# A residual's copy within DRAM, in one piece per image or in quarters, and an order account with two transfer queues

## The chip, the cores and the metric

The kernel runs on one core of a Trainium2 chip. The metric is the device time of one execution in microseconds. Before the change it is 3294.26 us, the median of three runs (3291.0 to 3302.8).

## The reference

Input x has 8 images of 256 channels and 32 x 32 positions, all in float32. Two layers follow each other.

```python
# layer 0, on the group-normalised x: convolutional attention
q = einsum("bchw,oc->bohw", x, q_w)                    # 8 heads of 32 channels, 1024 queries (and one global token)
kv = einsum("bchw,oc->bohw", x, kv_w)
ks, vs = (layernorm(pooled(t)) for t in split(kv))     # pooled: 4 sizes, 1024+256+121+25 = 1426 keys,
                                                       # each p + depthwise3x3(p)
att = softmax(q k^T * 32**-0.5) v
out = proj(att mixed over the channels of a head by a softmax made from the global token)
x = x + out                                            # the residual of layer 0
# layer 1, on the 1024 tokens of an image
t = t + softmax((LN(t) Wq)(LN(t) Wk)^T / 16) (LN(t) Wv)
t = t + sum_e w[f, e] * (relu(bn(relu(bn(LN(t) W1_e)) W2_e)) Wo_e)   # 8 experts; w: a softmax over experts
                                                       # of the mean over the images, for each token f
```

## The kernel before

`attention` computes layer 0 and the attention of layer 1; `experts` computes the experts. Both record every engine instruction through a class `Flow`, in one order per engine. That is why nearly all rows of the profile have one line, L670.

**The attention's main loop.** Layer 0 is a loop over 32 units: 8 images b, 2 groups c of four heads, 2 halves of the queries. A unit has 11 chunks kc of 128 keys; the last 18 keys of an image are taken together in one more step, so there are 360 steps in all. A step has four score matmuls into `sc` (one buffer, four PSUM banks), an exponential on ScalarE into a tile `pt` of 1 MB (six buffers), and, a step later, four matmuls into `pv`. For the softmax's denominator `add` sums two neighbouring `pt` tiles with an accumulating DMA that GpSimd (POOL) issues (`pt<-pt`, 160 of them), and `sums` on VectorE adds the pair into the unit's first pair, each half by itself. `unit`, a background thread, then normalises; after an image's last unit it starts `project`.

**The residual.** `t1[b]` is an image in DRAM. `prepare(b)`, which runs about one image ahead of the main loop, loads x[b] into SBUF (`xi`, two DMAs of 512 KB on SyncE's queue), has the copy x[b] to t1[b] issued within DRAM (1 MB, `t<-in_x_dram` in the profile) and goes on with the group norm, the pooling and the matmuls of keys, values and queries. `project(b)`, after the units of the image, adds its four quarters of 128 channels x 512 positions into t1[b] by accumulating DMAs from POOL (`t<-xr`). The last image has no such copy: `project` loads it and adds on VectorE. `layer1` then loads t1[b] (`t<-t`), and `outputs` reads it once more as its residual (`res<-t`).

**What sets the order.** `Flow` keeps an account: for each engine the time at which its last recorded instruction would end (`now`), for each tile when it is written (`ready`) and last read (`read`). `note` adds an instruction: it starts when its engine, its inputs and its output's readers allow it, lasts `cost`, and is seen by others `lag` later. Background threads (convolution, key and value tokens, projection, layer 1, its outputs) yield what they need next: an engine and tiles. `step` lets those go on whose tiles the account has ready within a few us of TensorE's time (`AHEAD`, `NEAR`), as long as a credit of matmul time per step lasts (`PACE`, `PACE1`); `finish` runs threads until a condition holds. So an estimate of a transfer's duration decides which instruction stands where on each engine, and the engines take them in this order. The chip itself waits for semaphores, not for the account.

A DMA's lag was a line for each queue: 2.0 us + 0.0045 us per KB on SyncE's, 1.5 us + 0.0078 us per KB on POOL's, whatever else was under way.

**After the attention.** While layer 1 of the last images and the gate of the experts (which needs all images) are still under way, `ahead` fills TensorE with first and second expert layers, whose results are stored in DRAM (`h<-h`) and fetched later. Expert layers of 256 x 256 weights are computed in seven products of 128 (`layer7`), except the first few, which are plain.

Of the kernel before, what the change touches and what calls it, by code (L numbers as in the profile page):

```python
# [14 lines left out]
DRAM = bass.MemoryType.DRAM  # L15

P = 128
# [7 lines left out]
NKC = 12  # L25
# [27 lines left out]
class Kit:  # L53


    def __init__(self, nc):
        self.nc = nc
        self.n = 0
# [598 lines left out]
class Flow:  # L657
# [27 lines left out]
    def __init__(self, tc, kit):  # L685
        nc = tc.nc
        self.tc, self.kit = tc, kit
        self.now = dict.fromkeys(("PE", "DVE", "ACT", "POOL", "SP"), 0.0)
        self.last = {}
        self.ready, self.read, self.writer, self.reader, self.slots, self.open = {}, {}, {}, {}, {}, set()  # L690
        self.pe = self.Engine(self, "PE", nc.tensor)
        self.ve = self.Engine(self, "DVE", nc.vector)
        self.act = self.Engine(self, "ACT", nc.scalar)
        self.pool = self.Engine(self, "POOL", nc.gpsimd)
        self.sp = self.Engine(self, "SP", nc.sync)
        self.threads = []
        self.cut = {}
        self.also = {}
        self.tiled = None
        self.columns = False  # L700
        self.credit, self.port = [0.0, 0.0], 0.0

    def tile(self, pool, shape, tag, bufs=1):
# [60 lines left out]
    def note(self, engine, op, ins, args, kwargs):  # L764
        aps = [a for a in (*args, *kwargs.values()) if hasattr(a, "tensor") or hasattr(a, "space")]
        out = kwargs.get("out", args[0] if args else aps[0])
        srcs = [a for a in aps if a is not out]
        prev = self.last.get(engine)
        if prev is not None:
            self.tc.add_manual_dep(  # L770
                ins.ins,
                prev,
                mybir.DependencyInfo(mybir.DependencyClass.NoSync, mybir.DependencyReason.DATA),
                reason="program order",
            )
        self.last[engine] = ins.ins.name
        start = self.now[engine]
        names = [n for a in srcs for n in self.keys(a)]
        outs = self.keys(out)
        for n in (*names, *outs):  # L780
            if self.writer.get(n) != engine:
                start = max(start, self.ready.get(n, 0.0))
        for o in outs:
            if self.reader.get(o, engine) != engine:
                start = max(start, self.read.get(o, 0.0))
        cost = self.cost(engine, op, out, srcs)
        if engine == "PE":

            tiling = None if op == "transpose" else self.tiling(srcs)
            if tiling != self.tiled:  # L790
                cost += {None: 0.2, "rows": 0.2, "columns": 0.13, "both": 0.2}[tiling]
                self.tiled = tiling

        wide = [a for a in srcs if a.space != PSUM and a.free_size() > 4]
        if "dma" not in op and engine == "POOL" or engine == "DVE" and wide and (len(wide) > 1 or op in ("tensor_scalar", "tensor_copy")):
            start = max(start, self.port)
            self.port = start + cost
        self.now[engine] = end = start + cost
        lag = 0.15
        if "dma" in op:  # L800
            size = 4e-3 * out.shape[0] * out.free_size() if out.space != DRAM else 4e-3 * srcs[0].shape[0] * srcs[0].free_size()
            lag = 2.0 + 0.0045 * size if engine == "SP" else 1.5 + 0.0078 * size
        for n in {*outs, self.key(out)}:
            self.ready[n] = max(self.ready.get(n, 0.0), end + lag)
            self.writer[n] = "DMA" if "dma" in op else engine
        self.open.difference_update(names)
        for n in {*names, *map(self.key, srcs)}:
            self.read[n] = max(self.read.get(n, 0.0), end + lag)
            self.reader[n] = engine

    @staticmethod
    def key(a):
# [85 lines left out]
def attention(tc, kit, f, outer, ended, nb, consts, x, t1, t2, hn, bounds, vecs, q_t, kv_t, proj_t, gqk_t, wqk, wqkv, vecs1, w1_d, w1c, gate_d, wrc, vecs2, bnvec):  # L898
# [6 lines left out]
    with ExitStack() as ctx:  # L905
        l1, shared = outer
        wp = ctx.enter_context(tc.tile_pool(name="w0", bufs=1))
        work = ctx.enter_context(tc.tile_pool(name="work0", bufs=1))
        psum = ctx.enter_context(tc.tile_pool(name="psum0", bufs=1, space=PSUM))

        def T(pool, shape, tag, bufs=1):
            return f.tile(pool, shape, tag, bufs=bufs)

        def small():
            if f.also and f.free("sx") < min(map(f.end, f.slots.get("sm", [None]))):
                return T(psum, [P, 512], "sx")
            return T(shared, [P, 512], "sm", bufs=2)
# [4 lines left out]
        def load_x(b):  # L922
            xi = T(work, [P, 2, HW], "xi")
            for k in range(2):
                f.sp.dma_start(xi[:, k, :], x[b, k * P : (k + 1) * P, :])
            return xi
# [147 lines left out]
        todo, done, read, freed, key_parts, normalised = [], [], [2], [0], [0], [0]  # L1074

        def pe(*tiles, tag=None):
            return "PE", tiles, tag

        def ve(*tiles):
            return "DVE", tiles, None  # L1080
# [10 lines left out]
        def until(cond):  # L1091
            return None, cond, None
# [270 lines left out]
        def prepare(b):  # L1363

            if b:
                yield until(lambda: len(asked) == 4)
            xi = xs.pop(b) if b in xs else load_x(b)
            if b < nb - 1:
                f.sp.dma_start(t1[b], x[b].rearrange("(k p) n -> p k n", p=P))
            st = T(work, [P, 2, 2, 6], "st")  # L1370
            mv = T(work, [P, 2, 2], "mv")
            for k in range(2):
                yield ve(xi[:, k, :])
                for h in range(2):
                    f.ve.bn_stats(st[:, k, h, :], xi[:, k, h * 512 : (h + 1) * 512])
                f.ve.bn_aggr(mv[:, k, :], st[:, k, :, :].rearrange("p h s -> p (h s)"))
            mean, var = mv[:, :, 0], mv[:, :, 1]
            yield pe(mv, tag="sm")
            gm = small()
            f.pe.matmul(gm[:, 0:2], lhsT=grp, rhs=mean, start=True, stop=True)  # L1380
            yield ve(gm)
            mu = T(work, [P, 2], "mu")
            f.ve.tensor_copy(mu, gm[:, 0:2])
            dev = T(work, [P, 2], "dev")
            f.ve.tensor_tensor(dev, mean, mu, ALU.subtract)
            f.ve.tensor_tensor(dev, dev, dev, ALU.mult)
            f.ve.tensor_tensor(dev, dev, var, ALU.add)
            yield pe(dev, tag="sm")
            gv = small()
            f.pe.matmul(gv[:, 0:2], lhsT=grp, rhs=dev, start=True, stop=True)  # L1390
            yield ve(gv)
            gr = T(work, [P, 2], "gr")
            rstd(gr, gv[:, 0:2], 1e-5)
            for k in range(2):
                yield ve(gr)
                f.ve.tensor_scalar(
                    xi[:, k, :], xi[:, k, :], mu[:, k : k + 1], gr[:, k : k + 1], ALU.subtract, ALU.mult
                )
            xl = T(work, [P, 2, NK - HW], "xl")
            if b == 0:  # L1400
                f.spawn(pool_levels(xi, xl), 2)
            else:
                yield from pool_levels(xi, xl)
            xp = xi, xl
            if b == 0:
                todo.extend([None] * 4)
                f.spawn(queries(b, xi), 3)
                yield from first_maps(xp)
            else:
                yield from maps(xp)  # L1410
            if b:
                yield from queries(b, xi)
            made[0] += 1
# [477 lines left out]
        for i in range(len(steps) + 1):  # L1891
            if i < len(steps):
                b, c, half, kc = steps[i]
                sl = slice(half * 512, half * 512 + 512)
                if kc % 4 == 0:
                    f.finish(lambda: key_parts[0] > 3 * b + kc // 4)
                if (half, kc) == (0, 0):
                    f.finish(lambda: (b, c) in qs and (b or (c, 0) in asked))
                    turn[0] = 2 * b + c
                    atts[b, c] = T(work, [P, HW], "att", bufs=2)  # L1900
                if i == 4:
                    f.finish(lambda: {0, 1}.issubset(whole))
                if b == 0 and kc == 0:
                    f.finish(lambda: (c, half) in asked)
                if kc == NKC - 1:
                    f.finish(lambda: key_parts[0] > 3 * b + 2 and (b, 1) in qs and (b or len(asked) == 4))
                    tail_scores(b)
                else:
                    pts[i] = scores(b, c, sl, kc)
                f.step()  # L1910
# [709 lines left out]
```

## Time and profile before

The profiled execution took 3300.42 us, and its span, from the first instruction to the last, is 3298.6 us.

| what | value |
|---|---|
| median of three runs | 3294.26 us |
| profiled execution, span | 3300.42 us, 3298.6 us |
| mean clock granted to TensorE | 0.978 |
| POOL's queue (q0): bytes, share of 16 engines' span | 179.85 MB, 28.1% |
| SyncE's queue (q1): bytes, share of 16 engines' span | 202.59 MB, 18.0% |
| exponentials pt<-sc | 352 of 1877 ns |
| additions pt<-pt on VectorE | 320 of 1220 ns in the median |
| pt<-pt on POOL, issue to landing | 7.9 us in the median of 160 |

A row of a table by stage has the stretch in us from the span's start, its length, each engine's busy time with the number of its instructions, the granted clock, the mean busy share of the 16 DMA engines and GB/s. A row of the waits names who waited for whom, the sum in us, the number of waits and the longest. A row of the groups gives the tile written and the tiles read (`pt<-sc`), without buffer numbers; one matmul of the program in float32 is two records.

### The profile page before, as it was taken

What the parts mean: (1) busy time and instruction counts of PE and PEld (TensorE: products, weight loads), DVE (VectorE), ACT (ScalarE), POOL (GpSimd) and SP (SyncE); (2) the same over time, 40 slices, a digit from 0 to 9 for tenths busy, and PEclk for the clock granted to TensorE, in tenths of its full rate; (3) what the DMA queues carried; (4) which work ended last, traced back from release to release, by engine and by line L of the source; (5) the groups of instructions that cost most, each with busy time, mean ns of one, the idle gap of its engine ahead of it and who ended that gap; (6) DMA issues with size and microseconds to landing.
All of it is one profiled execution on the core that took longest, in us unless ns stands there. A gap on an engine that the chain in (4) does not pass through costs nothing.

```text
span 3298.6 us, 55657 instructions
## 1 busy us (share of the span) xinstructions
PE 3093.2 (94%) x22264; PEld 1793.6 (54%) x22264; DVE 2466.9 (75%) x4060; ACT 1692.0 (51%) x2298; POOL 1174.7 (36%) x1269
## 2 busy tenths in 40 slices
PE   8787899989989979999999989999999999999998
PEld 4322234324334323343433447776888888888887
DVE  5787898888887878979754544444888888887776
ACT  4466667656666657566656423334333333344443
POOL 2212314122141141232121120002856555577776
PEclk9799999989999999999999999999999999999999
DMA  2358666665575565656576662214444344300000
GB/s 75 78 117 183 135 149 126 129 153 105 125 172 104 135 152 95 152 122 123 126 165 122 144 229 74 77 63 161 141 141 142 139 163 163 122 20 33 20 13 21
DMA packets 118524, 388.06 MB, mean 118 GB/s; under 512 B 14560, under 2 KB 40488, under 8 KB 95024
## 3 DMA queue, kind: packets, MB, share of 16 engines
q0 software_dynamic: 28608, 179.85, 28.1%
q1 hardware_dynamic: 86288, 202.59, 18.0%
q8 instruction: 177, 2.90, 0.4%
q10 hardware_dynamic: 3360, 1.97, 0.2%
q14 instruction: 91, 0.75, 0.1%
HBM read 125.03 MB, written 93.89 MB: 66 GB/s over the span
## 4 chain that ended last, share of the span: by engine, by line
PE 46%; DVE 4%; DMA 1%; ACT 1%; issue 1%; POOL 1%; SPq 0%; DVEq 0%; ACTq 0%; POOLq 0%
PE bank L670 21%; PE y L670 10%; PE sm L670 9%; PE sc L670 3%; PE pv L670 2%; PE sx L670 2%; DVE h L670 1%; DVE u L670 1%; DVE c L670 1%; ACT pt L670 1%; DVE t L670 0%; DMA pt<-pt 0%; DMA t<-t 0%; POOL t L670 0%; ACT h L670 0%
## 5 line engine op out<-in xcount | busy, mean ns | idle before, releaser
L670 ACT ACTIVATE pt<-sc 128x2048 f32<-128x2048 f32 x352 | 660.8, 1877 | 291.4 <-PE sc L670 226.4
L670 DVE SCALAR_TENSOR_TENSOR acc<-p,vec,acc 128x961 f32<-128x961 f32 (+3 forms) x960 | 565.0, 597 | 32.5 <-ACT acc L670 6.2
L670 PE MATMUL sc<-q,kn 32*128 32x512 f32 (+1 forms) x3072 | 425.4, 659 | 107.7 <-ACT pt L670 105.0
L670 DVE TENSOR_TENSOR pt<-pt,pt 128x1024 f32<-128x1024 f32 x320 | 391.1, 1267 | 125.3 <-DMA pt<-pt 92.7
L670 PE MATMUL pv<-pt,vt 128*32 128x512 f32 x2816 | 387.0, 622 | 0.0
L670 ACT ACTIVATE p1c<-bank 128x256 f32<-128x256 f32 x222 | 85.0, 383 | 562.5 <-PE bank L670 544.9
L670 ACT ACTIVATE h<-h,bnvec 128x512 f32<-128x512 f32 x444 | 335.7, 805 | 66.0 <-DVE h L670 58.2
L670 POOL TENSOR_TENSOR rstd<-rstd,mhalf 128x4 f32<-128x4 f32 (+2 forms) x88 | 107.0, 1216 | 734.6 <-DVE rstd L670 699.5
L670 POOL DMA_DIRECT2D pt<-pt x160 | 147.2, 920 | 565.7 <-ACT pt L670 399.2
L670 DVE TENSOR_TENSOR h<-p1c,bank 128x512 f32<-128x512 f32 x222 | 151.4, 682 | 217.2 <-PE bank L670 213.8
L670 PEld LDWEIGHTS sc<-q,kn 32*128 32x128 f32 (+1 forms) x3072 | 114.6, 180 | 303.2 <-ACT pt L670 198.3
L670 DVE TENSOR_TENSOR h<-u,bank 128x256 f32<-128x256 f32 (+1 forms) x444 | 226.1, 550 | 7.6
L670 POOL TENSOR_TENSOR tm<-h,tm 128x256 f32<-128x256 f32 x194 | 220.4, 1136 | 15.2
L670 PE MATMUL bank<-h,w2e 128*128 128x256 f32 (+1 forms) x636 | 215.6, 468 | 6.0 <-ACT h L670 3.4
L670 PEld LDWEIGHTS pv<-pt,vt 128*32 128x32 f32 x2816 | 56.1, 109 | 277.8 <-issue 264.8
L670 PE MATMUL sm<-p,v 128*32 128x256 f32 (+1 forms) x2328 | 200.2, 382 | 1.9 <-ACT sm L670 1.9
L670 DVE TENSOR_TENSOR h<-h,gate 128x1024 f32<-128x1024 f32 x128 | 196.0, 1531 | 0.5 <-ACT h L670 0.5
L670 POOL TENSOR_TENSOR tm<-h 128x512 f32<-128x512 f32 x97 | 129.8, 1338 | 181.4 <-ACT h L670 178.1
L670 PE MATMUL bank<-t,s1e 128*128 128x256 f32 x750 | 185.4, 383 | 5.5 <-DVE h L670 5.4
L670 PE MATMUL y<-t,s3e 128*128 128x256 f32 x768 | 187.0, 379 | 1.8 <-POOL t L670 1.8
L670 PE MATMUL sm<-y,t 128*32 128x256 f32 (+1 forms) x1872 | 178.7, 379 | 0.6 <-DVE st L670 0.6
L670 POOL TENSOR_TENSOR t<-h 128x512 f32<-128x512 f32 x100 | 129.7, 1297 | 131.8 <-DVE h L670 91.2
(317 smaller groups left out, 5506.9 us busy)
## 6 DMA issues: line engine op xcount, KB each, us to landing
pt<-pt POOLq DMA_DIRECT2D x160, 1024.0 KB, 7.9
h<-h SPq DMA_DIRECT2D x166, 512.0 KB
xi<-in_x_dram SPq DMA_DIRECT2D x16, 512.0 KB
t<-t SPq DMA_DIRECT2D x8, 1024.0 KB
res<-t SPq DMA_DIRECT2D x32, 256.0 KB
t<-res SPq DMA_DIRECT2D x32, 256.0 KB
hn<-res SPq DMA_DIRECT2D x32, 256.0 KB
hn<-hn SPq DMA_DIRECT2D x16, 512.0 KB
```

The source lines that it names most:

```text
L670: ins = fn(*args, **kwargs)
```

## The change

In `prepare` the copy x[b] to t1[b] is no longer issued. In the main loop, at step kc = 6 of each unit of images 0 to 6, a copy of the unit's quarter (128 channels of group c, 512 positions) is issued on SyncE's queue, ahead of that step's scores: 28 copies of 256 KB instead of 7 of 1 MB.

In the account, a DMA's lag comes from a new function `transfer`. It keeps the work left on two queues, POOL's and all others', in `left`, and the time up to which they were served in `served`. Both are served at half speed as long as both have work, one alone at full speed. A transfer has 0.0054 us of work per KB on POOL's queue or within DRAM, else 0.003; it is seen 1.7 us after its own queue's work, with as much of the other's as is served meanwhile, is done.

```diff
+        self.left, self.served = [0.0, 0.0], 0.0
         self.credit, self.port = [0.0, 0.0], 0.0
...
         if "dma" in op:
+            both = out.space == DRAM and srcs[0].space == DRAM
             size = 4e-3 * out.shape[0] * out.free_size() if out.space != DRAM else 4e-3 * srcs[0].shape[0] * srcs[0].free_size()
-            lag = 2.0 + 0.0045 * size if engine == "SP" else 1.5 + 0.0078 * size
+            lag = self.transfer(engine, end, size * (0.0054 if engine == "POOL" or both else 0.003))
...
+    def transfer(self, queue, at, work):
+
+        span = max(0.0, at - self.served)
+        self.served = max(self.served, at)
+        mine, other = queue == "POOL", queue != "POOL"
+        left = self.left
+        both = 2 * min(left)
+        done = min(span, both) / 2
+        for i in range(2):
+            left[i] = max(0.0, left[i] - done - max(0.0, span - both))
+        left[mine] += work
+        return 1.7 + left[mine] + min(left[mine], left[other]) + self.served - at
...
             xi = xs.pop(b) if b in xs else load_x(b)
-            if b < nb - 1:
-                f.sp.dma_start(t1[b], x[b].rearrange("(k p) n -> p k n", p=P))
...
+                if kc == NKC // 2 and b < nb - 1:
+                    f.sp.dma_start(t1[b][:, c, sl], x[b, c * P : (c + 1) * P, sl])
                 if i == 4:
                     f.finish(lambda: {0, 1}.issubset(whole))
```

## The prediction

> **What bounds the kernel now.** I read the page first, then a table by stage, the waits by stage, the stretches around the copies that are moved, and SyncE's queue there.
>
> From the page, the span and the busy times:
>
> ```profile
> span 3298.6 us, 55657 instructions
> PE 3093.2 (94%) x22264; PEld 1793.6 (54%) x22264; DVE 2466.9 (75%) x4060; ACT 1692.0 (51%) x2298; POOL 1174.7 (36%) x1269
> ```
>
> TensorE is the bound: the time is its work (3093 us) and what it idles (205 us). A change that adds no matmul can only move the idle part, and the speed of the matmuls. The table by stage (PE busy, PEld, DVE, ACT, POOL, clock, DMA share, GB/s) says where the idle part lies:
>
> ```profile
> 83.00:1876.00 1793.00, 1648.05 (x16022) 627.99 (x16024) 1427.73 (x2498) 1148.87 (x1382) 443.68 (x513) 0.97 0.61 132
> 1876.00:1916.00 40.00, 23.45 (x127) 12.55 (x119) 23.86 (x32) 5.33 (x11) 7.07 (x10) 0.91 0.55 159
> 1916.00:2290.00 374.00, 369.22 (x1418) 262.01 (x1419) 168.93 (x309) 137.50 (x234) 35.15 (x58) 0.99 0.32 112
> 2290.00:3299.00 1009.00, 984.72 (x4514) 857.38 (x4512) 797.59 (x1120) 365.34 (x602) 665.29 (x647) 0.99 0.28 96
> ```
>
> From the first exponential to the last (83 to 1876) TensorE idles 1793 - 1648 = 145 us; in the handover to the experts 17, after it 29. The change acts on the first. In the waits from 400 to 1900 us, what TensorE, ScalarE and VectorE stand still for (total, times, longest):
>
> ```profile
> PE sc L670 <- ACT pt L670: 65.3, 55, 4.7
> ACT pt L670 <- DMA pt<-pt: 24.3, 7, 5.9
> DVE pt L670 <- DMA pt<-pt: 75.4, 33, 8.9
> ```
>
> The scores wait for the exponential, because the tile sc has one buffer. Most of these waits are 1.0 us: a step in which no background matmul lies between the scores, so that ScalarE sets the pace (exponentials every 3.14 us of 1.88 us each, 1.26 us of hand-over). The long ones come from an exponential that waits for a pt buffer, which an accumulating DMA (pt<-pt) still holds. I looked for when. The five stretches of 35 us that begin with the copies of images 2 to 6 (t<-in_x_dram; those of images 0 and 1 go out at 1.65 and 37.67 us, before the first pt<-pt at 93.15), beside the five stretches before them; the two lines after the first sum are of the stretches before and after the inputs of image 7, which has no copy:
>
> ```profile
> 681.00:716.00 35.00, 24.50 (x146) 5.36 (x146) 25.54 (x34) 14.64 (x9) 4.83 (x6) 0.76 0.80 195
> 1150.00:1185.00 35.00, 28.55 (x286) 10.53 (x278) 27.08 (x43) 15.25 (x13) 6.64 (x7) 0.90 0.82 216
> sum 175.00, PE 143.53 PEld 49.80 DVE 135.00 ACT 94.63 POOL 41.45; mean PE 28.71 PEld 9.96 DVE 27.00 ACT 18.93 POOL 8.29
> ...
> 1330.00:1365.00 35.00, 35.00 (x352) 12.86 (x348) 31.00 (x54) 21.53 (x27) 6.00 (x6) 1.00 0.49 113
> 1365.00:1400.00 35.00, 34.27 (x350) 14.97 (x344) 33.93 (x57) 19.33 (x19) 9.04 (x12) 1.00 0.77 179
> ...
> sum 175.00, PE 166.01 PEld 55.49 DVE 147.87 ACT 105.22 POOL 22.08; mean PE 33.20 PEld 11.10 DVE 29.57 ACT 21.04 POOL 4.42
> ```
>
> With a copy TensorE is idle 31.5 us, before it 9.0: 22.5 us more in all, 4.5 for each copy. Where the inputs are loaded without a copy it idles 0.7 us. SyncE's queue at 680 us, and the median time of a pt<-pt from issue to landing, in 676:700 and then in 1360:1385:
>
> ```profile
> 680.21 0.32 SPq L670 DMA_DIRECT2D q<-hn  x1
> 680.62 0.88 SPq L670 DMA_DIRECT2D xi<-in_x_dram  x2
> 681.55 0.68 SPq L670 DMA_DIRECT2D t<-in_x_dram  x1
> ...
> pt<-pt POOLq DMA_DIRECT2D x3, 1024.0 KB, 13.6
> ...
> pt<-pt POOLq DMA_DIRECT2D x3, 1024.0 KB, 8.8
> ```
>
> So 2.5 MB go out within 2 us, the copy last, and the sums that run beside them take 13.6 us instead of 8.8.
>
> **What the Trainium skill says.** "DMA: Bandwidth & Descriptors", section "Issuing engines are not separate DMA queues": transfers of all issuing engines run on the same 16 DMA engines and interleave. The trace agrees: 13.6 us against 8.8. The same page, "Rules for kernel authors", asks for at least 1 MiB a DMA for the highest rate; the change goes the other way (256 KB), and no run here shows yet what that costs. "TensorE: Matmul & The Clock Gate", Part 1, says that the clock falls to half after an idle window: agrees, 0.76 granted in 681:716, after a wait of 4.7 us.
>
> **The change, part by part.**
>
> (1) Seven copies of 1 MB leave prepare; 28 of 256 KB stand at the middle step of the 28 units of images 0 to 6. By the page q1 moved 202.59 MB in 18.0% of 16 engines' 3298.6 us, or 2.9 us of all engines per MB. Five copies with sums beside them: 14.7 us of engine time leave the bursts. They come back in parts of 0.73 us, where a sum alone takes 7.0 us and one is due every second step (every 11 us on average: 1793 us for 160); some hidden delay, then. What TensorE gains is between 0 (the burst's other 1.5 MB do the harm) and the 22.5 us above. I take half, 11 us: the stretch at 1365 speaks for more, but is one, and lay where background matmuls stood ready. The clock in the five stretches was 0.90, 1.00, 0.76, 1.00, 0.90, before them 0.95 once: (0.44 - 0.05) x 35 = 14 us of clock lost. TensorE waits for ScalarE there, so I take 0 and keep 10 as the other end. 21 more issues on SyncE at 0.4 to 0.7 us are 12 us of a queue that mostly waits. A copy waits for nothing itself, but stands behind SyncE's waits in order. Behind the last quarter of an image on POOL stand project's accumulates (t<-xr), and behind those the next pt<-pt: see rival D.
>
> (2) The account. No instruction is added, but its estimates decide the order. For a pt<-pt it had 1.5 + 0.0078 x 1049 KB = 9.7 us; now 1.7 + 0.0054 x 1049 = 7.4 alone and more when SyncE's queue has work; SyncE's 256 KB go from 3.2 to 2.5 us. The trace's 6.9 alone and 7.9 in the median are nearer to the new figures. I counted what the built orders hold. Matmul prices from the trace: 0.86 us for 128x512, 0.43 for 128x256, a quarter for each 32-wide part. Work after the last scores: 1365 us before, 1349 after (-16); it holds 4 fewer plain layers of 4 x 0.86 and 4 more of 7 x 0.43, which is -1.7. Work of background matmuls between the first and the last scores: 874 before, 888 after (+14). Images of layer 1 brought forward: 24 of 32 outputs are done before the last scores instead of 23.
>
> What +14 costs in the attention depends on where it lies. For each of the 359 steps I took the larger of its matmul work and of its ScalarE work (row durations) + 1.26 us. The sum is 1772 us for the old order, against 1793 between the exponentials in the trace, so the count is good to about 1%. For the new order it is 1795: +23. By image, before and after: 215/213, 216/225, 224/236, 234/241, 228/241, 253/222, 224/233, 177/185. Steps without background: 59 and 60. The tail is 98% busy on TensorE, so its -16 counts in full. Net of the order: +23 - 16 = +7, with an error of some 9 (as much as images moved against each other).
>
> (3) The handover stays: the same loads stand in the same places of SyncE's queue between the last image's projection and the first expert, so its wait of 10.4 us for hn<-hn remains.
>
> Sum against the profiled execution (3300.42 us, of which the span is 3298.6): +7 - 11 = -4, so 3296. The median of the runs shown, 3294.26, is 6 us lower, and so the forecast is 3290.
>
> **The rivals.**
>
> A, the forecast: collisions give 11, the order takes 7: **3290**. For it speaks that TensorE's total work is the same within 2 us.
>
> B, faster: the copies were the whole cause, and the clock goes with them. -22.5 - 10 + 7 = -25: **3269**. For it: 0.7 us of idle at image 7. Against it: q<-hn and xi stay in the burst, and the order brings new coincidences that cannot be read beforehand.
>
> C, slower: VectorE becomes the bound in images 3 and 4. The new order puts 221 and 222 us of VectorE work before the end of those images' last normalisations, where the old one had 200 and 209 (+34). VectorE was busy 190 of 227 us and 184 of 230 in the stretches of these images, so there is cover of 37 and 46 us. If its idle time, which is waits inside chains (75 us of it for pt<-pt), does not shrink, the 34 come in full, where the count of steps had 20 for them: +14. Late sums then hold pt buffers, and the 11 us are gone. 3294 + 7 + 14 = **3315**. It decides once the two images together need over 500 us.
>
> D: the change doesn't do what it says, since SyncE issues in order: its longest wait is 70.7 us for res, and quarters behind such a wait go out in bunches (in six places of the new order at most one other transfer stands between two quarters). The last quarter then lands after project is ready, POOL waits, and the sums behind it too. Six pt buffers cover some 10 us. At 5 us for each of four images: 3294 + 7 + 20 = **3321**.
>
> **How the numbers follow.** 0.5% is 16.5 us, about what a measurement of this kernel can tell from no change: below 3278 is faster, above 3311 slower. A 0.40 (3270 to 3310 with the error of the order and 0 to 22 us of relief), B 0.28, C 0.24, D 0.08. A reaches over its limits at both ends by about 0.03. So faster 0.31, within 0.34, slower 0.35. The range goes from 3258 (B with the order 9 better than counted) to 3325 (just past D). The likeliest case has 3270 to 3310 beside it.
>
> **What would show it.** Step 1 is right if the five stretches after the input loads have PE busy near 33 of 35 us instead of 28.7, the clock above 0.95 at each, and no pt<-pt over 11 us there; wrong if 13 us remain with xi and q<-hn alone. Step 2: the last exponential near 1876 + 23 - 11 = 1888, and 16 us less from there to the end; the h<-h issues fall from 166 to 142. C shows as images 3 and 4 longer than 241 each and VectorE's busy share above 0.9. D shows as POOL waiting for t<-in_x_dram before t<-xr. The prediction is wrong if the attention moves by over 20 us either way, which the order's details can do.

## The result, and the profile after

The changed kernel takes 3242.89 us in the median of 4 runs (3236.82 to 3246.57); the ratio to the kernel before is 0.9838, with a 95% interval of 0.9813 to 0.9862. The kernel before, taken beside it, has a median of 3294.7 us in 4 runs, so the change brings 52 us. The forecast was 3290 us with a range down to 3258, so the time lies outside the range, on its fast side.

The profiled execution took 3236.82 us, its span is 3235.0 us, 63.6 us less than the span before. Some 12 us of that are the two executions' own luck: the one before lay 6 us above its median, this one 6 us below. The page after, its span and busy times:

```profile
span 3235.0 us, 55827 instructions
PE 3064.9 (95%) x22342; PEld 1793.5 (55%) x22342; DVE 2458.7 (76%) x4064; ACT 1692.2 (52%) x2302; POOL 1198.6 (37%) x1293
```

TensorE's busy time fell by 28.3 us and its idle time by 35.3. Its work is the same: the order of instructions has 1.7 us less of it. So the busy part is speed. The mean granted clock rose from 0.978 to 0.989. The trace records when TensorE ran at half speed. Laid over its busy time, these records cost 55 us before and 30 after.

The table by stage of the changed kernel. The stages are start, attention (first to last exponential), handover to the first expert, layer 1's rest beside the experts, and experts; the columns are as before (PE, PEld, DVE, ACT, POOL, clock, DMA share, GB/s):

```profile
0.00:84.00 84.00, 68.48 (x194) 34.06 (x194) 48.90 (x106) 35.14 (x72) 23.42 (x42) 0.98 0.16 49
84.00:1855.00 1771.00, 1642.31 (x16174) 636.64 (x16177) 1427.99 (x2528) 1150.30 (x1387) 448.50 (x520) 0.98 0.63 136
1855.00:1893.00 38.00, 34.18 (x130) 20.79 (x122) 16.87 (x16) 8.65 (x16) 3.24 (x6) 0.96 0.47 128
1893.00:2211.00 318.00, 316.93 (x1234) 226.86 (x1235) 153.46 (x280) 119.10 (x205) 32.15 (x56) 0.99 0.36 129
2211.00:3235.00 1024.00, 1003.02 (x4618) 875.13 (x4616) 811.53 (x1139) 379.04 (x623) 691.25 (x671) 1.00 0.24 83
```

The same table of the kernel before, cut at the ends of the same stages, so that the stages can be compared:

```profile
83.00:1878.00 1795.00, 1650.05 (x16054) 629.00 (x16056) 1429.73 (x2499) 1150.61 (x1382) 445.68 (x514) 0.97 0.61 132
1878.00:1916.00 38.00, 21.45 (x99) 11.54 (x91) 21.86 (x31) 3.59 (x10) 5.07 (x9) 0.91 0.58 167
1916.00:2292.00 376.00, 371.22 (x1427) 263.78 (x1428) 170.90 (x312) 139.05 (x236) 35.15 (x58) 0.99 0.32 114
2292.00:3299.00 1007.00, 982.72 (x4505) 855.62 (x4503) 795.62 (x1117) 363.79 (x599) 665.29 (x647) 0.99 0.28 95
```

The attention is 24 us shorter, although it holds 14 us more of background matmuls: it idles 129 us instead of 145, and loses less clock. The handover lasts 38 us in both, but TensorE works in 34 of them instead of 21. The rest is 41 us shorter (1342 instead of 1383). The h<-h issues fell from 166 to 142, by the two pages.

The waits from 400 to 1900 us, after (the prediction has the same rows of before):

```profile
PE sc L670 <- ACT pt L670: 61.9, 70, 2.8
ACT pt L670 <- DMA pt<-pt: 22.4, 9, 4.6
DVE pt L670 <- DMA pt<-pt: 93.9, 41, 8.0
```

The sum of the first row hardly changed (65.3 us before), but its shape did: there are more waits, and none is over 2.8 us where there were some up to 4.7. VectorE's waits for the sums grew, from 75.4 us to 93.9. From the start to the end of the handover, TensorE's waits of more than 1.3 us came to 101 us in 34 pieces before and are 59 us in 20 pieces now; the shorter ones went from 74 to 87 us.

Last, the five stretches of 35 us after the loads of xi, after the change:

```profile
713.00:748.00 35.00, 34.66 (x348) 16.74 (x340) 31.45 (x71) 21.93 (x28) 6.74 (x9) 1.00 0.80 190
1132.00:1167.00 35.00, 29.66 (x226) 11.19 (x219) 31.87 (x46) 19.30 (x17) 6.40 (x7) 0.95 0.94 223
sum 175.00, PE 158.12 PEld 64.21 DVE 148.00 ACT 106.36 POOL 43.73; mean PE 31.62 PEld 12.84 DVE 29.60 ACT 21.27 POOL 8.75
```

TensorE is busy 158.1 of 175 us there instead of 143.5. That is close to what step 1 of the prediction had named as its sign. The experiments show that the moved copies are not its cause.

### The profile page after: what moved, and what is told of

Its sections match the earlier page's. It is cut to its first block, busy times and chain, and to the rows that moved or that the text cites. A ratio compares the mean times of both kernels' runs of the same rounds, so it can differ in the third digit from the quotient of the medians.

```text
span 3235.0 us, 55827 instructions
## 1 busy us (share of the span) xinstructions
PE 3064.9 (95%) x22342; PEld 1793.5 (55%) x22342; DVE 2458.7 (76%) x4064; ACT 1692.2 (52%) x2302; POOL 1198.6 (37%) x1293
## 3 DMA queue, kind: packets, MB, share of 16 engines
q0 software_dynamic: 28608, 179.85, 28.7%
## 4 chain that ended last, share of the span: by engine, by line
PE 71%; DVE 10%; ACT 7%; DMA 4%; issue 4%; POOL 2%; ACTq 0%; DVEq 0%; POOLq 0%; SPq 0%
PE bank L670 22%; PE sm L670 17%; PE y L670 10%; PE sc L670 8%; PE sx L670 8%; PE pv L670 6%; ACT pt L670 5%; DMA pt<-pt 3%; DVE acc L670 3%; DVE rec L670 1%; DVE pt L670 1%; DVE h L670 1%; DMA pt<-ptail 1%; DVE c L670 1%; DVE u L670 1%
## 5 line engine op out<-in xcount | busy, mean ns | idle before, releaser
L670 DVE SCALAR_TENSOR_TENSOR acc<-p,vec,acc 128x961 f32<-128x961 f32 (+3 forms) x960 | 554.9, 586 | 32.0 <-ACT acc L670 6.4
L670 PE MATMUL sc<-q,kn 32*128 32x512 f32 (+1 forms) x3072 | 417.3, 644 | 102.0 <-ACT pt L670 97.9
L670 PE MATMUL pv<-pt,vt 128*32 128x512 f32 x2816 | 380.1, 612 | 0.1
L670 POOL TENSOR_TENSOR tm<-h,tm 128x256 f32<-128x256 f32 x202 | 234.7, 1162 | 15.8
L670 DVE TENSOR_TENSOR h<-u,bank 128x256 f32<-128x256 f32 x452 | 230.2, 550 | 7.8
L670 PE MATMUL bank<-h,w2e 128*128 128x256 f32 (+1 forms) x620 | 203.6, 457 | 2.8 <-DVE h L670 1.9
L670 DVE TENSOR_TENSOR u<-h,bank 128x512 f32<-128x512 f32 x226 | 155.5, 688 | 24.7 <-DVE h L670 0.9
```

The costliest lines, as they stand in the source:

```text
L670: ins = fn(*args, **kwargs)
```

## The experiments

**Order and copies apart.** The account decides the order, and the copies are instructions. To part them, `note` got a form in which the account counts a transfer without issuing one, and `follow`, which puts an uncounted instruction into SyncE's order. All engines but SyncE then keep their order exactly. Each run has the kernel before beside it on the same chip (medians of 3296 to 3298 us), and the ratios are to those. The expectations name theories: 'collisions' (the copies beside the sums cost the time), 'order' (the new order won it), and later 'accuracy' (the new account orders better because it is nearer to the chip), 'lottery' (any change of an estimate draws another order, good or bad by chance) and 'sharing helps' (accounts in which the two queues share the engines order better). The core of the edits, here for the old order with quarters:

```diff
-        prev = self.last.get(engine)
-        if prev is not None:
...
-        self.last[engine] = ins.ins.name
+        if ins is not None:
+            self.follow(engine, ins)
...
             if b < nb - 1:
-                f.sp.dma_start(t1[b], x[b].rearrange("(k p) n -> p k n", p=P))
+                f.note("SP", "dma_start", None, (t1[b], x[b].rearrange("(k p) n -> p k n", p=P)), {})
...
+                if kc == NKC // 2 and b < nb - 1:
+                    f.follow("SP", nc.sync.dma_start(t1[b][:, c, sl], x[b, c * P : (c + 1) * P, sl]))
```

Old order, quarters:

> Every engine's instructions stand in the order of the kernel before; only on SyncE's queue the 7 whole copies are replaced by 28 quarters at the middles of the units (the account still counts the whole copies). Theory 'collisions' (the copies beside the sums cost most of what the change won): about 3250 us, PE busy over 160 of 175 us in the five stretches after the input loads. Theory 'order' (the new account's order won it): 3280 to 3290 us, 5 to 15 us below before. The prediction's own term was 11 us.

Measured: 3296.78 us, ratio 0.9999 (0.9988 to 1.0011). Nothing was gained; both theories had expected some gain. This order is also the one that the kernel before gets when the quarters alone are put in with the old account: counting them moves no instruction of another engine. So the first half of the change, by itself, does nothing.

For the next one all copies of images 1 to 6 go out at once, right after the loads of image 1:

```diff
+            for i in ((0,), range(1, nb - 1))[b] if b < 2 else ():
+                f.follow("SP", nc.sync.dma_start(t1[i], x[i].rearrange("(k p) n -> p k n", p=P)))
```

Old order, copies early:

> As before in every engine's order, but the copies of images 1 to 6 all go out right after the inputs of image 1, at about 38 us, before the first accumulating DMA: no copy runs beside a sum. It bounds what copies can cost in the old order. 'Collisions': at or below the run with quarters, 3245 to 3255 us. 'Order': 3275 to 3288 us.

Measured: 3294.53 us, ratio 0.9997 (0.9988 to 1.0005). With no copy beside any sum the old order takes what it took, so this is above the range of either theory again. The stretches that the prediction blamed on the copies, in this kernel:

```profile
681.00:716.00 35.00, 25.66 (x154) 5.51 (x154) 26.16 (x34) 15.62 (x9) 5.78 (x7) 0.76 0.73 166
1150.00:1185.00 35.00, 26.98 (x252) 9.77 (x244) 25.02 (x37) 13.96 (x13) 5.74 (x6) 0.90 0.76 192
sum 175.00, PE 144.52 PEld 50.50 DVE 134.61 ACT 96.41 POOL 39.86; mean PE 28.90 PEld 10.10 DVE 26.92 ACT 19.28 POOL 7.97
```

144.5 us busy, against 143.5 with the copies: the idle time stayed where it was when its supposed cause was taken away. ScalarE's timeline at the first of them tells what happens there (start, duration, instruction, idle time before it and what ended it):

```profile
681.24 1.88 ACT L670 ACTIVATE pt<-sc 128x2048 f32<-128x2048 f32 x1 [0.32 <-PE sc L670]
684.38 1.88 ACT L670 ACTIVATE pt<-sc 128x2048 f32<-128x2048 f32 x1 [1.26 <-PE sc L670]
687.52 1.88 ACT L670 ACTIVATE pt<-sc 128x2048 f32<-128x2048 f32 x1 [1.26 <-PE sc L670]
695.27 1.88 ACT L670 ACTIVATE pt<-sc 128x2048 f32<-128x2048 f32 x1 [5.87 <-DMA pt<-pt]
700.74 1.88 ACT L670 ACTIVATE pt<-sc 128x2048 f32<-128x2048 f32 x1 [3.59 <-DMA pt<-pt]
```

Exponentials follow each other every 3.14 us, with hardly any other matmul between the scores, until one waits 5.87 us for a sum. Two exponentials give a sum every 6.28 us. By the page of before, q0 took 28.1% of the 3298.6 us for 179.85 MB, so a sum of 1.05 MB needs an estimated 5.4 us of all engines. That leaves 0.9 us to spare in such a run of steps, and the inputs and the queries that still come there (1.57 MB, an estimated 4.6 us at 2.9 us per MB) are more than that. In this kernel the three pt<-pt from 676 to 700 us still took 13.3 us in the median, from issue to landing, against 13.6 with the copy. So the copy is not what makes these sums late. In two other stretches the sum beside the loads lands some 2 us earlier without the copy (9.9 us after its issue instead of 12.0 at 484, 8.3 instead of 10.7 at 922), and still the kernel takes the same time. That the inputs make the sums late is an estimate; no run here moves them. The copy stood at that place because `prepare` issues it where it loads xi.

New order, whole copies:

> Every engine's instructions stand in the order of the changed kernel; on SyncE's queue the quarters are replaced by whole copies at the places where the kernel before had them, after the loads of xi. 'Collisions': 3280 to 3295 us, most of the gain lost. 'Order': 3250 to 3260 us, 11 us or so above the changed kernel.

Measured: 3239.6 us, ratio 0.9836 (0.9815 to 0.9858): the whole gain, with the copies where they had been. It is more than either theory gave. So the quarters themselves aren't needed for the gain; the order is.

New order, copies early:

> The order of the changed kernel, with the copies of images 1 to 6 at about 38 us, ahead of all sums. It shows what the quarters in the middles of the units still cost: both theories 3235 to 3245 us, that is 0 to 8 us below the changed kernel's 3243; more if 20 MB-long quarters beside sums hurt.

Measured: 3237.71 us, ratio 0.9828 (0.9808 to 0.9848). It is the lowest median of all runs, but its interval and that of the changed kernel overlap for the most part; that it beats the changed kernel isn't shown.

**Parts of the account.** The order is the whole gain. Which part of the account makes it? First the new account alone, without the quarters:

> The new account with the copies whole and in prepare, as before. Both theories left (the order is the whole gain; copies beside sums cost nothing) give 3235 to 3255 us. If the quarters' place in the account matters for the order: above 3265.

Measured: 3268.58 us, ratio 0.9924 (0.99 to 0.9948): half the gain. The quarters matter after all, as entries of the new account: without them the order is another one, 26 us slower. Then the old account with one of its two lines replaced:

```diff
-            lag = 2.0 + 0.0045 * size if engine == "SP" else 1.5 + 0.0078 * size
+            lag = 2.0 + 0.0045 * size if engine == "SP" else 1.7 + 0.0054 * size
```

> The kernel before with one number pair of its account changed: a DMA of POOL's queue is seen 1.7 us + 0.0054 us per KB after its issue (7.4 us for a pt<-pt) instead of 1.5 + 0.0078 (9.7 us). No two queues, SyncE's line as before. Theory 'accuracy' (the estimate of the sums' landing was 2 us too long, and the order suffers from that): half the gain or more, 3245 to 3270 us. Theory 'lottery' (any change of an estimate draws another order, and the changed kernel drew a good one): anything from 3240 to 3310, without relation to the others. The hole before the first expert, 10 us, stays in this order, as no matmul of layer 1 stands behind the last projection.

Measured: 3308.35 us, ratio 1.0038 (1.0022 to 1.0054), slower. And SyncE's line:

```diff
+            lag = 1.7 + 0.003 * size if engine == "SP" else 1.5 + 0.0078 * size
```

> The kernel before with SyncE's line of the account alone changed: 1.7 us + 0.003 us per KB instead of 2.0 + 0.0045. 'Accuracy': little of the gain, 3275 to 3298 us, since few background threads wait for SyncE's transfers. 'Lottery': 3240 to 3310.

Measured: 3303.24 us, ratio 1.0016 (1.0007 to 1.0025). POOL's line came nearer to what the trace shows. The account counts the lag from the end of the issuing instruction, to which it gives 1 us more; counted so, a sum of the kernel before takes 6.0 us alone and 7.0 in the median (the prediction's 6.9 and 7.9 count from the start of the issue), and the lag is 7.4 us instead of 9.7. SyncE's line came nearer only in its slope (2.9 us per MB by the page; the profile has no landings for SyncE's transfers). Both lose, and 'accuracy' had both wrong. The control, 0.1 us more on both lines:

```diff
+            lag = 2.1 + 0.0045 * size if engine == "SP" else 1.6 + 0.0078 * size
```

> A control: the kernel before with 0.1 us more for every DMA in the account, on both queues. No better an estimate, yet the order of all engines is another one: 30 us more of matmul work stands between the first and the last scores. 'Accuracy': like before, 3285 to 3305 us. 'Lottery': more than 15 us away from before, or as fast as the changed kernel.

Measured: 3280.1 us, ratio 0.9957 (0.9943 to 0.997). A tenth of a microsecond in an estimate, for no reason, gains 14 us by the ratio (17 by the medians), as 'lottery' had it. That is more than the prediction had allowed for the error of the order (9 us).

**How wide the draw is.** So the same was done to the new account (its 1.7 us became 1.8, 1.6, 1.5 and 1.75), to the new account without the term for the other queue's work, and to the old one with 0.1 us less:

```diff
-        return 1.7 + left[mine] + min(left[mine], left[other]) + self.served - at
+        return 1.7 + left[mine] + self.served - at
```

Fixed part 1.8 us, with sharing:

> The changed kernel with 1.8 us instead of 1.7 for a transfer's fixed part in the new account. Theory 'accuracy' (the new account orders better because it is nearer to the chip): 3235 to 3265 us, as the estimate is as good. Theory 'lottery': anything between 3240 and 3310, on average near 3285; behind the last projection this order has no matmul of layer 1, so the hole before the first expert (10 us and its half-speed clock) should be back.

Measured: 3258.43 us. It fits both theories. The hole is back: TensorE waits 11.45 us before the first expert.

Fixed part 1.6 us, with sharing:

> The changed kernel with 1.6 us instead of 1.7. As new_plus: 'accuracy' 3235 to 3265, 'lottery' 3240 to 3310. The hole should be back here too, as only 4 short transposes stand behind the last projection.

Measured: 3281.68 us, outside 'accuracy'. The hole is back (10.43 us).

Fixed part 1.7 us, without sharing:

> The changed kernel with the term for the other queue's work left out of the lag. 'Accuracy' of the sharing: worse than new_plus and new_minus by 10 us or more, 3270 to 3310. 'Lottery': within the scatter of those two, above or below.

Measured: 3290.38 us, 32 and 9 us above the two runs before; neither description fits quite.

The old account, 0.1 us less:

> The kernel before with 0.1 us less for every DMA (1.9 and 1.4). 'Accuracy': 3285 to 3305. 'Lottery': 3240 to 3310. Its order leaves more layer-1 work behind the attention (22 outputs done instead of 23), 12 us more of tail work.

Measured: 3290.84 us. It fits both.

Fixed part 1.5 us, with sharing:

> The changed kernel with a fixed part of 1.5 us. 'Sharing helps' (accounts in which the two queues share the engines order better on average, with a scatter of 15 us): 3240 to 3285. 'Lottery alone': 3240 to 3310, as often above 3280 as below.

Measured: 3280.07 us. It fits both.

Fixed part 1.75 us, with sharing:

> The changed kernel with a fixed part of 1.75 us. 'Sharing helps': 3240 to 3285. 'Lottery alone': 3240 to 3310. VectorE's waits for pt<-pt, 107 to 121 us in the shared accounts so far, stay below 130.

Measured: 3287.08 us, 2 us above the range of 'sharing helps'. VectorE's waits for pt<-pt, counted from 100 us on as in the expectation, were 108 us.

Fixed part 1.6 us, without sharing:

> The account without the other queue's work, fixed part 1.6 us. 'Sharing helps': 3280 to 3315, and VectorE waits for pt<-pt 140 us or more, as its additions stand too early. 'Lottery alone': 3240 to 3310.

Measured: 3292.86 us, as 'sharing helps' had it, but with 138 us of VectorE's waits, just under the 140 expected.

Fixed part 1.8 us, without sharing:

> The account without the other queue's work, fixed part 1.8 us. Here the order happens to have, as the changed kernel's, 24 matmuls of layer 1 between the last projection and the first expert, and 1349 us of work after the last scores. 'Sharing helps': 3270 to 3300 in spite of that. 'Lottery alone' with the tail as its part that can be read beforehand: 3240 to 3265.

Measured: 3274.47 us, in the range of 'sharing helps' and 9 us above the range that the tail alone would give.

All of them, sorted by their medians. Attention is from the first to the last exponential, rest from there to the end, both from the trace. The work behind the last scores and the matmuls of layer 1 behind the last projection are read from the built order. The runs come from several chips, so the ratio to the kernel before is the safer column.

| account | median us | ratio | attention | rest | work behind the last scores | matmuls behind the projection |
|---|---|---|---|---|---|---|
| new: changed kernel | 3242.89 | 0.9838 | 1771 | 1381 | 1349 | 24 |
| new, 1.8 | 3258.43 | 0.9888 | 1801 | 1372 | 1337 | 0 |
| new, copies whole | 3268.58 | 0.9924 | 1807 | 1376 | 1349 | 24 |
| unshared, 1.8 | 3274.47 | 0.9925 | 1813 | 1378 | 1349 | 24 |
| new, 1.5 | 3280.07 | 0.9946 | 1801 | 1396 | 1349 | 12 |
| old + 0.1 | 3280.1 | 0.9957 | 1816 | 1379 | 1333 | 4 |
| new, 1.6 | 3281.68 | 0.9961 | 1786 | 1408 | 1357 | 4 |
| new, 1.75 | 3287.08 | 0.9977 | 1802 | 1407 | 1354 | 0 |
| unshared, 1.7 | 3290.38 | 0.9981 | 1800 | 1408 | 1357 | 4 |
| old - 0.1 | 3290.84 | 0.9986 | 1780 | 1426 | 1377 | 13 |
| unshared, 1.6 | 3292.86 | 0.9986 | 1804 | 1411 | 1355 | 0 |
| old: kernel before | 3296 | 1 | 1795 | 1421 | 1365 | 1 |
| old, SyncE's line new | 3303.24 | 1.0016 | 1800 | 1426 | 1363 | 0 |
| old, POOL's line new | 3308.35 | 1.0038 | 1851 | 1374 | 1337 | 0 |

Three things follow. First, small steps of one constant move the time by up to 44 us within the new account (3243 with 1.7 us, 3287 with 1.75), and no time is near another because its constant is near. Second, the six accounts with sharing have a mean of 3270 us, the eight without 3292. But the changed kernel isn't a draw like the others: it was there before them. Without it the other five with sharing have 3275, and the three that lack only the sharing 3286: 11 us of difference, beside a scatter of about the same size in each group. That the sharing helps is not shown by so few draws. Third, the changed kernel lies 27 us below its own account's mean. That part of its gain is the luck of this one order.

The sharing does have a trace in VectorE's waits for the sums, here of the run with POOL's line new, then of the new account without sharing (1.7), from 400 to 1900 us:

```profile
DVE pt L670 <- DMA pt<-pt: 150.5, 61, 8.2
...
DVE pt L670 <- DMA pt<-pt: 133.3, 51, 15.1
```

They were 75.4 us in the kernel before and 93.9 in the changed one. In the kernel before, 66 of the 160 sums landed more than 7.4 us after the issuing instruction, and 13 more than the old account's 9.7 us. So an estimate of 7.4 us for every sum puts many of VectorE's additions ahead of their sums, and VectorE, which takes its work in order, stands still. But these waits don't follow the time: the kernel before has the second lowest of all, and the fastest of the unshared draws (1.8) 95.1 us. They aren't what makes the changed kernel fast.

**The handover.** In the changed kernel, 24 score matmuls of layer 1 stand between the last projection and the first expert. They go there in a loop of `experts` that steps the background threads until the first weights are there. Without it:

```diff
-        for _ in range(NE):
-            f.step((PACE2, PACE2))
-            if max(f.ready[a.name] for a in (w1[0], xs[0])) <= f.now["PE"]:
-                break
```

> The changed kernel without the loop that fills TensorE with layer 1 until the first expert's weights are there: the 24 score matmuls of layer 1 that stood between the last projection and the first expert come after it; everything up to the last projection is unchanged, total matmul work is 0.4 us less. It prices the filled hole: if it is worth what the hole of the kernel before showed (10 us of waiting, and half-speed clock after it), 10 to 15 us above the changed kernel. If later waits shrink in exchange: 0 to 5.

> The changed kernel on the same chip and beside the same runs of before, for the comparison with new_no_fill: 3238 to 3248 us.

Measured: 3253.71 us without the loop (3251 to 3260) and 3242.49 us for the changed kernel on the same chip (3238 to 3245), so the filled hole is worth 11 us. TensorE's timeline in the kernel before, in the changed one without the loop, and in the changed one:

```profile
1899.67 5.50 PE L670 MATMUL sm<-att,mt 128*128 128x512 f32 x12 [2.82 <-DVE st L670]
1905.01 0.59 PE L670 MATMUL sm<-diag,con 128*128 128x256 f32 x2
1915.98 5.22 PE L670 MATMUL bank<-hn,w1e 128*128 128x512 f32 x8 [10.38 <-DMA hn<-hn]
...
1878.91 1.88 PE L670 MATMUL sx<-att,mt 128*128 128x512 f32 x4
1892.37 6.64 PE L670 MATMUL bank<-hn,w1e 128*128 128x512 f32 x8 [11.58 <-DMA w2e<-in_w_dram]
...
1880.76 1.88 PE L670 MATMUL sx<-att,mt 128*128 128x512 f32 x4
1882.47 10.52 PE L670 MATMUL sm<-y,t 128*128 128x256 f32 x48
1893.22 7.11 PE L670 MATMUL bank<-hn,w1e 128*128 128x512 f32 x16 [0.23 <-issue]
```

Without the loop the first expert waits 11.58 us for a transfer. In the changed kernel it starts at nearly the same moment (1893.2 us against 1892.4), and 10.5 us of other work are done by then.

## Why the prediction was wrong

**"I take half, 11 us" (step 1) was wrong by all of it.** The relief is 0, with both ends of the interval within 0.12%. The step went wrong where it read the 22.5 us of additional idle time beside the copies as caused by them. They were beside the copies because both come where an image's preparation begins: with the copies gone from there, TensorE was busy 144.5 us of the 175 instead of 143.5. The stretch at image 7, taken as the control, differed in more than the copy: it had background matmuls. The prediction says so and still leans on it. The sizes did not fit either: a copy is about 3 us of the DMA engines' time by the page, while in the stretch at 681 TensorE idled 10.5 us.

**"Net of the order: +23 - 16 = +7, with an error of some 9" (step 2) is the step that sets the miss.** Measured, the order brings -52 us in the median, and the 14 orders lie over 65 us. In the profiled executions the attention, forecast at +23, came at -24, and what follows it, forecast at -16, at -40. The counts of work in it were good: the work behind the last scores, the work brought into the attention, the h<-h issues. What failed is the sum of steps as a time.

The same count, redone over the two traces with the prediction's prices, gives 1774 and 1797 us, for 1793 and 1769 between the first and the last exponential. That the first pair agrees to 1% was luck. In the kernel before, steps that took longer than their count add up to 150 us, and steps that took less to 131; in the changed kernel it is 126 and 154. So the larger of the two kinds of work is no lower bound for a step. Most steps that fell short by over 0.3 us (93 of 107 before, 104 of 125 after) are such in which ScalarE's work plus the 1.26 us of hand-over was the larger, and nearly all have other ScalarE work beside the exponential. The hand-over was added there, but it seems to pass beside that work.

By image the count was right about images 5 (253 to 222 us, measured 252 to 210) and 1 (216 to 225, measured 205 to 221) in sign and about in size. It was wrong about images 2 and 4, which were to grow by 12 and 13 us and changed by -3 and +2, and image 0 fell by 13 us instead of 2.

By kind, the -63.6 us of the profiled executions are: idle time in the attention -16, in the handover -13, in the rest -7, and speed -27 (of the busy time's -28.3 all but the work's 1.7). The speed is partly the two executions' luck: three profiles in the old order lose 44 to 52 us of the attention to half speed, four in the new one 25 to 33, about 18 us less.

**The clock was "0, with 10 as the other end".** It was tied to the copies, and came at about -18 us in the attention with the order. It goes with the long waits: the Trainium skill's page "TensorE: Matmul & The Clock Gate", Part 1, has the clock halved after an idle window, and the traces agree. In the attention of the kernel before, 12 of the 21 waits of TensorE of 1.9 us or more have half speed beside them (it begins in them or within 1 us after), and 1 of the 50 of about 1 us (0.9 to 1.3). In the changed kernel there are 12 of the long waits, 6 of them with half speed, and none of 59 of the short. The page puts the window at about 3.4 us; here waits of 1.9 to 2.5 us had half speed beside them too. No run here changes the waits without the order.

**"The handover stays" (step 3) was wrong.** The loads do stand in the same places of SyncE's queue, and the first expert does start as long after the last projection as before (10.8 us then, 10.6 now). But what TensorE has to do meanwhile was not looked up, though the built order tells it: 1 matmul behind the last projection before, 24 after. This could have been read, and the run without the loop prices it at 11 us.

**The rivals.** B had the right sign and the wrong cause. C did not come: images 3 and 4 took 235 us each, 470 together and not over 500. VectorE was busy 409 of these 470 us, where it had been 392 of 464. D did not come either: POOL has no wait that t<-in_x_dram ended.

**The signs.** "PE busy near 33 of 35 us" after the loads came near (31.6), and proved nothing, since the order had changed too; with the copies removed and the old order kept, it was 28.9. A sign that two causes would give doesn't tell them apart. The other half of it, no pt<-pt over 11 us there, did not come: the medians of those issued within 25 us of 923 and of 1132 us are 11.1 and 11.4. The sign against step 1, 13 us with xi and q<-hn alone, did: 13.3 with the copies out of the way. "The last exponential near 1888" began at 1853, and "16 us less from there" was 40 less. The attention moved by more than the 20 us that the prediction had named as its own limit. One sum of the prediction is off by 2 us: B with the order 9 us better is 3260, not 3258.

## What to carry to other kernels

Where an estimate decides the order of instructions, a change of the estimate is a new draw. Before crediting it to its better fit, change the same constant by a meaningless amount a few times: here that alone moved the time by up to 44 us. Idle time that lies beside a transfer is tested by moving the transfer with the order held fixed. And a handover between stages is worth a look at what stands behind the last instruction of the old stage: here the wait itself stayed as long, but it could be filled.

## What was not expected of the hardware

Moving the seven copies of 1 MB within DRAM changed nothing measurable in this kernel: whole beside the sums, in quarters, or six at once at 38 us, the ratios were 0.9997 to 1 in the old order and 0.9828 to 0.9838 in the new. The intervals leave room for some 4 us in the old order and 8 in the new, and no run leaves the copies out altogether. This was so although the DMA engines were busy 61% of the attention, and although an accumulating transfer takes an estimated 5.4 us of all engines where, in the fastest steps, one is due every 6.28 us.
